# Sums of layer 0 on GpSimd, another join for the last image, and side work that starts only while TensorE has room in a tile

## The chip, the cores and the metric

The kernel runs on one core of a Trainium2 chip. A core has five engines that run their own instruction streams and wait for each other through semaphores: TensorE (PE in the profile, its weight loads PEld), VectorE (DVE), ScalarE (ACT), GpSimd (POOL) and SyncE (SP), whose queue issues the DMA transfers. SBUF is the working memory of 128 partitions; PSUM is the memory that TensorE writes, eight banks of 128 x 512 f32. The metric is the time of one execution on the device in microseconds, the median of several runs. The kernel before takes 18407.37 us, the median of three runs between 18365.60 and 18408.36 us.

## The reference

Four images of 64 x 64 pixels with 96 channels go through four layers. Each layer is `x = x + conv(ln(x))` and then `t = t + ffn(ln(t))`. The "convs" are recurrences along the 4096 pixels of an image.

Layer 0 projects the normalised pixel to a value, a gate, a delta and three sets A, B, C of 96 x 16 numbers, and runs

```python
def step(h, ins):
    A_t, B_t, C_t, d_t, u_t, g_t = ins
    d = d_t[..., None]
    h_new = d * (A_t * h) + d * (B_t * u_t[..., None])
    y = g_t * jnp.sum(C_t * h_new, axis=-1)
    return (h_new, y)
```

so that the sum over the 16 states of a channel, times the gate, is projected to the output. Layers 1 to 3 are selective scans over four orders of the pixels (rows, columns, and both reversed) with 192 inner channels and 16 states:

```python
dA = jnp.exp(dl[..., None] * A)
h = dA * h + (dl * u_l)[..., None] * b_l[:, :, None, :]
y = jnp.einsum('bkdn,bkn->bkd', h, c_l)
...
y = ys[:, 0] + jnp.flip(ys[:, 2], axis=-1) + wh_back(ys[:, 1]) + wh_back(jnp.flip(ys[:, 3], axis=-1))
y = _layernorm(y, out_norm_w, out_norm_b)
y = y * jax.nn.silu(z)
return jnp.einsum('bhwd,cd->bhwc', y, out_proj_w)
```

The sum of the four orders is called the join below. The inputs u and z of a scan come from a projection, a 3 x 3 depthwise convolution and a silu. The ffn multiplies in fp8 with a hidden width of 384.

## The kernel before

**Layer 0** is the function `gated`. An image is cut into 8 strips of 512 pixels, a strip has 12 tiles `i` of 128 rows (32 channels x 4 states; `g` is one of three groups of 32 channels, `q` one of four sets of 4 states). For each tile TensorE projects A and B into one double PSUM bank (`project`, tile name `bc`) and later C into another (`project_c`, PSUM name `c`); VectorE makes the two factors and runs the scan (`recur`); ScalarE copies C with its bias to SBUF, and GpSimd multiplies it with the scan's result (`times_c`, SBUF name `c`). After every three tiles (one `q`, all `g`) `accumulate` has TensorE add the products of 4 states into the PSUM tile `sum`, one matmul with the constant `fold` per tile; after the fourth such round `finish` takes the sum. While tiles are made, the generator `prepare` makes the next strip's normalisation, transposes (`l_xt`) and small projections, three steps per tile, on all engines. From the second image on, the work between layer 0 and layer 1 for image 0 runs beside it as a job.

**The scans** of layers 1 to 3 are the function `scans`. There are 12 stages (3 layers x 4 images), called stage 0 to stage 11 here. A stage has 24 items (2 directions x 4 segments of 1024 pixels x 3 chunks of 128 rows) of 16 states, so 384 tiles of 128 x 1024. For tile `k` VectorE multiplies `bc` (the B row, spread over partitions by TensorE with `sel`, `b_rows`) by `du` and runs the scan to `h`; ScalarE makes the decay `da` two tiles ahead; GpSimd multiplies `h` by the C row `c` that a DMA has brought; TensorE adds the products of tile `k - 3` into `acc` (`accumulate`). For the three states of `ON_POOL` per item GpSimd makes the product that VectorE makes otherwise (tile name `e`), and then VectorE has the scan alone. The double bank `bc` has two buffers, `h` three, `c` six.

**Jobs.** What lies between two layers of an image (`between`: join, norm, gate, output projection, ffn; and then for the next layer the input projection and the convolution) is a Job: generators called chains, three for the first half (`feeds`, `mixers`, `joins`) and two for the second (`convolves`, `takes`). One step of the job, a link below, advances each chain of the current round to its next `yield`. In each scan tile `beside` runs between VectorE's product and its scan, and calls `work`, which adds `rate` to the job's credit and starts as many links as the credit pays. The job of the next image in the stage must be done at tile 356 of 384 of the stage, else it is run to its end there. All jobs stand in one list and run one after another. After layer 3 three images have their ends (`between(im, 3, im.dst)`, first half only) beside the scans, and the last image has its end alone, after all scans, with six PSUM banks.

**Order.** `InOrder` chains every engine's instructions in the order in which the program writes them, so an engine that waits holds all that was written behind. In a tile the order is: carry and decays on ScalarE, `b_rows(k + 1)` on TensorE, `times_c(k - 1)` on GpSimd, VectorE's product, the side work, the scan, then `accumulate(k - 3)` and `keep_busy`. `InOrder` also counts the columns that TensorE streams. `late` in `scans` is the program's own running count of columns by which TensorE is behind, against `FITS` = 7600 columns for a usual tile and `FITS_SHORT` = 4600 for one of `ON_POOL`; before the change it only decides how many dummy matmuls (`keep_busy`, `nothing`) go in.

**The join** (`join_orders`) makes a strip's 512 pixels from four pieces by matmuls with `ident`: per 128 pixels one of `yr`, two of `cols_a`, one of `yc` and four of `part_c`, added up in PSUM. The profile has all helper-issued instructions at line 102, so they are told apart by tile names here. An f32 matmul of the program stands as two in the profile, a transpose as one.

Of the kernel before, what the change touches and what calls it, by code (L numbers as in the profile page):

```python
# [18 lines left out]
HW = 64  # L19
L = HW * HW  # L20
# [109 lines left out]
def metaformer(ctx: ExitStack, tc: tile.TileContext, x, l0_ab, l0_rest, ssm, ffn, out):  # L130
# [227 lines left out]
    def join_orders(im, s, hold):  # L358
# [37 lines left out]
        yield from norm.measure(yt, DI, 1e-5)  # L396
        hold["y", s] = yt, norm

    def mixer_out(im, layer, s, hold):

        w = weights[layer].w
        yt, norm = hold.pop(("y", s))
        zl, zh, xr = load_z(im, s)
        yield from norm.settle()
        yield
        normalise(yt, yt, DI, norm.r, norm.nm)
        yield
        yield True
        g = []
        for i, (a, b, z) in enumerate(((0, 128, zl), (128, 192, zh))):  # L410
            ps = bank("y_c")
            transpose_strip(ps, yt, a, b)
            yield
            v = sb(1, f"u{i}", [128, MM])
            m = b - a
            sc, bias = (w[0:m, W_LN + 2 * i + k : W_LN + 2 * i + k + 1] for k in range(2))
            act.activation(v[0:m], ps[0:m], AF.Identity, bias=bias, scale=sc)
            release()
            yield i == 0
            g.append(v)  # L420
            if i == 0:
                continue
            for v, z, m in ((g[0], zl, 128), (g[1], zh, 64)):
                pool.tensor_tensor(v[0:m], v[0:m], z[0:m], ALU.mult)
                yield
        yield True
        ps = bank("out_proj")
        for q in range(G):
            t = slice(128 * q, 128 * q + 128)
            o = ps[:, C * q : C * q + C]  # L430
            pe.matmul(o, g[0][:, t], w[:, W_OUT : W_OUT + C], start=True, stop=False)
            pe.matmul(o, g[1][0:64, t], w[0:64, W_OUT + C : W_OUT + 2 * C], start=False, stop=True)
            yield
        yield
        x1 = sb(2, "x1", [128, G, C])
        dve.tensor_tensor(x1, xr, ps[:, 0 : G * C].rearrange("p (g c) -> p g c", g=G), ALU.add)
        release()
        yield
        norm = Norm()
        yield from norm.measure(x1, C, 1e-5)  # L440
        hold["x", s] = x1, norm
# [225 lines left out]
    def between(im, layer, dst=None):  # L667


        hold = {"in": {}, "pads": {}, "z": {}}  # L670
        new = dram.tile([L // G, G * C], F32, tag="x", name="x") if dst is None else dst

        def columns():
            return sb(1, "cols_a", [128, L]), sb(1, "part_c", [128, L // 2])

        def first():
            if layer:
                cols_a, part_c = hold["cols"] = columns()
                sp.dma_start(out=cols_a[0:64], in_=im.y[1, 64:128, :])
                sp.dma_start(out=cols_a[64:128], in_=im.y[0, 64:128, :])  # L680
                for k in range(2):
                    sp.dma_start(
                        out=part_c[64 * k : 64 * k + 64],
                        in_=im.y[2, 64:128, k * L // 2 : (k + 1) * L // 2],
                    )
                load_y(im, 0, hold)
            for _ in range(9 if layer else 3):
                yield

        yield [Chain(first())]  # L690
        done = {"y": 0, "x": 0, "end": 0}

        def joins():
            for s in range(NSTRIP):
                yield lambda: done["x"] > s - 2
                yield True
                yield from join_orders(im, s, hold)
                done["y"] += 1

        def mixers():  # L700
            for s in range(NSTRIP):
                yield lambda: done["end"] > s - 2 and (layer == 0 or done["y"] > s)
                if layer:
                    yield from mixer_out(im, layer, s, hold)
                else:
                    yield from measure_x(im, s, hold)
                done["x"] += 1

        def feeds():
            for s in range(NSTRIP):  # L710
                yield lambda: done["x"] > s
                yield from feed_forward(im, layer, s, hold, new)
                done["end"] += 1

        yield [Chain(f()) for f in (feeds, mixers, joins)[: 3 if layer else 2]]
        if dst is not None:
            return

        def second():
            if layer + 1 not in weights:  # L720
                weights[layer + 1] = Weights(layer + 1)
                for _ in range(4):
                    yield
                weights[layer + 1].derive()
                for t in range(0, 15, 3):
                    yield
                    weights[layer + 1].derive_taps(range(t, t + 3))
            im.x = new
            im.u = dram.tile([3, 128, L], F32, tag="u", name="u")
            im.z = dram.tile([DI, L], F32, tag="z", name="z")  # L730
            hold["cols"] = columns()
            hold["in"][0] = load_x(im, 0)
            yield
            yield

        yield [Chain(second())]
        done = {"in": 0, "out": 0}

        def takes():
            for s in range(NSTRIP):  # L740
                yield lambda: done["out"] > s - 3
                yield from take_in(im, layer + 1, s, hold)
                done["in"] += 1

        def convolves():
            yield lambda: done["in"] > 0
            gate_z(im, 0, hold)
            exp_and_ln()
            yield
            yield  # L750
            store_z(im, 0, hold)
            for s in range(NSTRIP):
                yield lambda: done["in"] > min(s + 1, NSTRIP - 1)
                yield True
                yield from convolve(im, layer + 1, s, hold)
                done["out"] += 1

        yield [Chain(f()) for f in (convolves, takes)]

    class Job:  # L760
# [3 lines left out]
            self.rounds, self.rate, self.credit = rounds, rate, 0.0  # L764
            self.chains, self.done, self.round = [], False, -1

        def step(self):
            rate = self.rate[min(self.round, 3)] if isinstance(self.rate, tuple) else self.rate
            self.credit = min(self.credit + rate, 3.0)
            while self.credit >= 1 and not self.done:  # L770
                self.credit -= 1
                while not self.done and all(c.done for c in self.chains):
                    self.chains = next(self.rounds, None)
                    self.round += 1
                    self.done = self.chains is None
                if self.done:
                    break
                for c in self.chains:
                    pump(c)
# [95 lines left out]
    def scans(stages, jobs, pac):  # L875
# [157 lines left out]
        b_from_dram(ON_POOL[0])  # L1033
        working = []

        def work():

            while working and working[0].done:
                working.pop(0)
            if working:  # L1040
                working[0].step()

        late = 0
        for k in range(last + 5):
            q, n = divmod(k, NS)
            if k <= last:
# [7 lines left out]
                if item.chunk == 1 and n == 4 and at(q + 2) is not None:  # L1054
                    if q % per == per - 2:
                        for job in jobs[q // per][:1]:
                            while not job.done:
                                work()
                                settle()
                    segment = Chain(next_segment(items[q + 2 : q + 5]))  # L1060
                if n == 8 and nxt is not None:
# [49 lines left out]
            late = max(0, late + int(pe.columns - begun) - (FITS_SHORT if on_pool(k) else FITS))  # L1111
            settle()
        while working:
            work()
            settle()


    def gated(images, job, pac):
# [158 lines left out]
        def times_c(t):  # L1277
            st, i, h = t["st"], t["i"], t["h"]
            act.copy(st.carry[:, i : i + 1], h[:, MM - 1 : MM])
            c = sb(6, "c", [128, T])[:, 0:MM]  # L1280
            act.activation(c, t["c"], AF.Identity, bias=col(2 * LT + i))
            pool.tensor_tensor(c, h, c, ALU.mult)
            t["h"] = c

        def accumulate(three):

            for t in three:
# [2 lines left out]
                    acc[32 * g : 32 * g + 32],  # L1290
                    fold,
                    t["h"],
                    start=q == 0,
                    stop=q == LQ - 1,
                    tile_position=(0, 32 * g),
                )

# [31 lines left out]
        for k in range(len(tiles) + 2):  # L1329
# [5 lines left out]
                times_c(made[k - 1])  # L1335
            if k > LG and (k - 2) % LG == LG - 1:
                three = [made.pop(j) for j in range(k - 1 - LG, k - 1)]
                accumulate(three)
                if three[-1]["i"] == LT - 1:
                    drain(ending, help_job)  # L1340
                    ending = Chain(finish(three[-1]["st"]))
            for c in (ending, ahead, ahead, ahead):
# [13 lines left out]
    with tc.tile_pool(name="pbig", bufs=2, space=bass.MemoryType.PSUM) as wides_pool:  # L1356
# [5 lines left out]
        for at in range(len(stages)):  # L1362
            jobs.append([])
            if at + 1 < len(stages):
                im, layer = stages[at + 1]
                jobs[-1].append(Job(between(im, layer - 1), (1.75, 1.75, 1.4, 1.4)))

            for im in {10: images[:2], 11: images[2:3]}.get(at, ()):
                jobs[-1].append(Job(between(im, 3, im.dst), 2.6))
        with tc.tile_pool(name="pac", bufs=1, space=bass.MemoryType.PSUM) as pac:  # L1370
            scans(stages, jobs, pac)

# [119 lines left out]
```

## Time and profile before

| | |
|---|---|
| median of three runs | 18407.37 us (18365.60 to 18408.36) |
| profiled execution, its own time | 18376.11 us |
| its span | 18374.3 us |
| layer 0 (to the first scan of stage 0) | about 0 to 1805 us |
| stages 0 to 11 | 1805 to 18160 us |
| the last image's end | 18160 to 18374 us |
| busy, share of the span | DVE 90%, PE 87%, POOL 81%, ACT 59% |

A stage of the scans lasts 1340 to 1370 us, and the last one, stage 11, 1483 us (16677 to 18160). The time that counts in a stage is VectorE's: 312 tiles with a product of 1208 ns and a scan of 2344 ns, and 72 tiles with a scan of 2327 ns. An idle time is attributed in the profile to the instruction that ended it ("bc <- PE bc": VectorE's product waited for TensorE's rows). Idle time of an engine that nobody waits for costs nothing.

### The profile page before, as it was taken

How to read it: one execution, taken by the hardware profiler on the slowest of the kernel's cores; microseconds unless marked ns; L12 is line 12 of the kernel's file. 1: busy time of each engine (PE TensorE's matmuls, PEld its weight loads, DVE VectorE, ACT ScalarE, POOL GpSimd, SP SyncE). 2: the span in 40 equal slices, each digit the busy share in tenths (PEclk: the TensorE clock that was granted, in tenths of full speed). 3: DMA queues.
4: the chain of work that ended last, by engine and by line, in shares of the span. 5: the costliest groups of instructions: out<-in, count | busy, mean ns of one | idle time of the engine just before them, and what ended most of it. 6: DMA issues, size and time to landing. Idle time of an engine off the chain costs nothing. (4 is left out here: it accounts for less than half of the span.)

```text
span 18374.3 us, 238128 instructions
## 1 busy us (share of the span) xinstructions
PE 15921.8 (87%) x76325; PEld 5026.5 (27%) x76325; DVE 16459.7 (90%) x12586; ACT 10918.2 (59%) x18201; POOL 14853.6 (81%) x9319
## 2 busy tenths in 40 slices
PE   8898798798898888898898898898898898888887
PEld 3333222222222322322322222222222222223333
DVE  6756999899999999999999999999999999998885
ACT  3443565565664665665665665665665665666664
POOL 3433888888888988988988988988888988988885
PEclk8998999899899999899999999998899999998887
DMA  2212788788789889889889898898899899898885
GB/s 52 51 48 65 196 220 219 196 223 218 196 224 227 209 220 229 207 226 229 212 224 226 212 228 223 214 225 221 213 230 221 211 228 223 215 230 205 198 213 138
DMA packets 1276076, 3658.88 MB, mean 199 GB/s; under 512 B 287760, under 2 KB 333040, under 8 KB 1268688
## 3 DMA queue, kind: packets, MB, share of 16 engines
q1 hardware_dynamic: 1274256, 3642.86, 79.6%
q8 instruction: 615, 10.08, 0.3%
q14 instruction: 629, 5.15, 0.1%
q10 hardware_dynamic: 576, 0.79, 0.0%
HBM read 3271.50 MB, written 320.86 MB: 196 GB/s over the span
## 5 line engine op out<-in xcount | busy, mean ns | idle before, releaser
L102 POOL TENSOR_TENSOR c<-h,c 128x1024 f32<-128x1024 f32 (+1 forms) x4992 | 11309.7, 2276 | 3032.2 <-DVE h L102 800.2
L102 DVE TENSOR_TENSOR_SCAN h<-da,carry,bc 128x1024 f32<-128x1024 f32 x3744 | 8776.2, 2344 | 558.2 <-POOL c L102 114.6
L102 PE MATMUL acc<-c,twice 64*64 64x512 f32 x36864 | 5449.6, 667 | 77.6 <-POOL c L102 76.9
L102 DVE TENSOR_TENSOR bc<-du,bc 128x1024 f32<-128x1024 f32 x3744 | 4524.2, 1208 | 331.6 <-PE bc L102 294.1
L102 ACT ACTIVATE da<-delta,decay 128x1024 f32<-128x1024 f32 x3744 | 4272.6, 1144 | 534.2 <-DVE h L102 531.2
L102 PE MATMUL bc<-bs,sel 96*128 96x512 bf16 x7488 | 2417.4, 407 | 1708.0 <-DVE h L102 1661.2
L102 ACT COPY carry<-h 128x1 f32<-128x1 f32 x3456 | 654.3, 190 | 3693.1 <-DVE h L102 3683.3
L102 DVE TENSOR_TENSOR_SCAN h<-bc,carry,e 128x1024 f32<-128x1024 f32 x864 | 2010.8, 2327 | 90.4 <-POOL e L102 64.9
L102 POOL TENSOR_TENSOR e<-du,e 128x1024 f32<-128x1024 f32 x864 | 2039.3, 2360 | 60.1 <-DMA e<-cs 59.8
L102 PE MATMUL acc<-sel,nothing 96*128 96x512 bf16 x7653 | 2025.8, 396 | 0.0
L102 PEld LDWEIGHTS acc<-c,twice 64*64 64x64 f32 x36864 | 1063.9, 140 | 2562.3 <-issue 1800.5
L102 PEld LDWEIGHTS <-sel 96*128 96x128 bf16 x7488 | 479.4, 99 | 4560.9 <-DVE h L102 2881.5
L102 ACT ACTIVATE bc<-delta,decay 128x1024 f32<-128x1024 f32 x864 | 963.0, 1115 | 955.7 <-DVE h L102 757.9
L102 PEld LDWEIGHTS <-nothing 96*128 96x128 bf16 x7653 | 646.1, 100 | 1996.7 <-issue 1492.8
L102 ACT ACT_TABLE_LOAD x857 | 1099.5, 1283 | 15.4 <-PEq L1485 0.7
L102 PE MATMUL conv<-pad,tap_lo 128*128 128x512 f32 x1728 | 888.2, 611 | 0.0
L102 ACT ACTIVATE c<-c,l_bias 128x512 f32<-128x512 f32 x384 | 263.8, 687 | 786.2 <-PE c L102 774.3
L102 POOL TENSOR_TENSOR du<-delta,u 128x1024 f32<-128x1024 f32 x288 | 679.9, 2361 | 38.0 <-DMA c<-cs 35.7
L102 PE MATMUL dt_proj<-rows,w 12*128 12x512 f32 x1152 | 670.8, 663 | 1.2 <-ACT hq L102 0.6
L102 PE MATMUL x_proj<-u,xp 128*108 128x512 f32 x1152 | 624.0, 653 | 45.3 <-DMA u<-u 14.2
L102 PE MATMUL conv<-pad,tap_hi 128*128 128x512 f32 (+1 forms) x1152 | 615.3, 630 | 0.0
L102 DVE TENSOR_TENSOR_SCAN h<-da,l_carry,bc 128x512 f32<-128x512 f32 x384 | 491.5, 1280 | 41.5 <-DVE bc L102 1.9
(151 smaller groups left out, 14174.4 us busy)
## 6 DMA issues: line engine op xcount, KB each, us to landing
c<-cs SPq DMA_DIRECT2D x9216, 256.0 KB, 5.5
e<-cs SPq DMA_DIRECT2D x1728, 256.0 KB, 4.8
u<-u SPq DMA_DIRECT2D x288, 512.0 KB, 7.4
y<-y SPq DMA_DIRECT2D x1152, 128.0 KB, 3.4
y<-y SPq DMA_DIRECT2D x144, 512.0 KB, 7.5
xr<-x SPq DMA_DIRECT2D x224, 192.0 KB, 5.8
u<-u SPq DMA_DIRECT2D x288, 128.0 KB, 4.6
pad<-y SPq DMA_DIRECT2D x288, 128.0 KB, 6.1
```

Source lines behind the costliest of these rows:

```text
L102: ins = f(*a, **k).ins
```

## The change

- `times_c` of layer 0 adds the four products of a group on GpSimd into two SBUF tiles that live for the strip (`st.sums`); `accumulate` runs once per strip, with three matmuls instead of twelve.
- The last image's end uses `join_alone`: VectorE adds the pieces in SBUF, reading `cols_a` and `part_c` across, and TensorE transposes the sums, eight transposes per strip. The second half of `part_c` is loaded into two `u` tiles instead, at partitions 0 to 63.
- The other images' ends move: image 0's is listed behind stage 9 (before: 10), image 1's behind stage 10, image 2's behind stage 11 as before.
- A job's link in the scans starts only while `late`, the tile's columns so far and 2048 columns for `accumulate` are within `FITS` or `FITS_SHORT`; credit that is not spent is kept up to 5 (before 3). Where the program waits for a job to end, the limit is off.
- Rates go from 1.75 and 1.4 links per tile (first and second half) to 2.2 and 1.7, in stages 9 and 10 to 2.6 and 2.4, and for the ends from 2.6 to 2.8.

```diff
+    def join_alone(im, s, hold):
+        yr, yc = hold["in"].pop(s)
+        if s + 1 < NSTRIP:
+            load_y(im, s + 1, hold)
+        cols_a, part_c = hold["cols"]
+        rows = slice(SR * s, SR * s + SR)
+        def across(v):
+            return v.rearrange("p (c r) -> p r c", r=HW)[:, rows, :]
+        def along(v):
+            return v.rearrange("p (r c) -> p r c", c=HW)
+        dve.tensor_tensor(along(yr), along(yr), across(cols_a), ALU.add)
+        c0 = 0
+        for v in [part_c[0:64]] + [u[0:64] for u in hold["rest"]]:
+            w = v.shape[1] // HW
+            part = along(yc)[:, :, c0 : c0 + w]
+            dve.tensor_tensor(part, part, across(v), ALU.add)
+            c0 += w
+        yield
+        yt = sb(2, "yt", [128, G, DI])
+        for pair in range(2):
+            ps = bank("y_t")[:, 0 : 2 * DI].rearrange("p (g c) -> p g c", g=2)
+            for g in range(2):
+                t = slice(128 * (2 * pair + g), 128 * (2 * pair + g) + 128)
+                pe.transpose(ps[:, g, 0:128], yr[:, t], ident)
+                pe.transpose(ps[:, g, 128:DI], yc[:, t], ident[0:64, 0:64])
+            yield
+            act.copy(yt[:, 2 * pair : 2 * pair + 2, :], ps)
+            release()
+            yield pair == 0
+        norm = Norm()
+        yield from norm.measure(yt, DI, 1e-5)
+        hold["y", s] = yt, norm
...
+        alone = dst is not None and im is images[-1]
...
-                for k in range(2):
+                for k in range(1 if alone else 2):
                     sp.dma_start(
                         out=part_c[64 * k : 64 * k + 64],
                         in_=im.y[2, 64:128, k * L // 2 : (k + 1) * L // 2],
                     )
+                if alone:
+                    hold["rest"] = [sb(4, "u", [128, T]) for _ in range(2)]
+                    for k, u in enumerate(hold["rest"]):
+                        t = L // 2 + k * T
+                        sp.dma_start(out=u[0:64], in_=im.y[2, 64:128, t : t + T])
...
-                yield from join_orders(im, s, hold)
+                yield from (join_alone if alone else join_orders)(im, s, hold)
...
-        def step(self):
+        def step(self, full=lambda: False):
             rate = self.rate[min(self.round, 3)] if isinstance(self.rate, tuple) else self.rate
-            self.credit = min(self.credit + rate, 3.0)
-            while self.credit >= 1 and not self.done:
+            self.credit = min(self.credit + rate, 5.0)
+            while self.credit >= 1 and not self.done and not full():
...
-        def work():
+        def work(hurry=False):
             while working and working[0].done:
                 working.pop(0)
             if working:
-                working[0].step()
+                working[0].step((lambda: False) if hurry else crowded)
+
+        def crowded():
+            most = FITS_SHORT if on_pool(k) else FITS
+            return late + int(pe.columns - begun) + 4 * MM > most
...
                             while not job.done:
-                                work()
+                                work(True)
...
             act.copy(st.carry[:, i : i + 1], h[:, MM - 1 : MM])
-            c = sb(6, "c", [128, T])[:, 0:MM]
+            g, q = divmod(i, LQ)
+            if i == 0:
+                st.sums = [sb(6, "c", [128, T]) for _ in range(2)]
+            total = st.sums[g // 2][:, g % 2 * MM : g % 2 * MM + MM]
+            c = total if q == 0 else sb(6, "c", [128, T])[:, 0:MM]
             act.activation(c, t["c"], AF.Identity, bias=col(2 * LT + i))
             pool.tensor_tensor(c, h, c, ALU.mult)
-            t["h"] = c
+            if q:
+                pool.tensor_tensor(total, total, c, ALU.add)
+            t["h"] = total
...
-                    start=q == 0,
-                    stop=q == LQ - 1,
+                    start=True,
+                    stop=True,
...
-                accumulate(three)
                 if three[-1]["i"] == LT - 1:
+                    accumulate(three)
                     drain(ending, help_job)
...
-                jobs[-1].append(Job(between(im, layer - 1), (1.75, 1.75, 1.4, 1.4)))
-            for im in {10: images[:2], 11: images[2:3]}.get(at, ()):
-                jobs[-1].append(Job(between(im, 3, im.dst), 2.6))
+                jobs[-1].append(Job(between(im, layer - 1), (2.6, 2.6, 2.4, 2.4) if at >= 9 else (2.2, 2.2, 1.7, 1.7)))
+            for im in {9: images[:1], 10: images[1:2], 11: images[2:3]}.get(at, ()):
+                jobs[-1].append(Job(between(im, 3, im.dst), 2.8))
```

More of the change, by code (lines that the diff above doesn't have):

```diff
@@ L1113, in scans @@
         while working:
-            work()
+            work(True)
             settle()
```

## The prediction

> **What bounds the kernel now.** First the busy time by stretches (duration, busy us and instruction counts of PE, PEld, DVE, ACT and POOL, granted TensorE clock, DMA share, GB/s): layer 0, stages 0 to 2, 3 to 9, 10, 11, the last image's end.
>
> ```profile
> 0.00:1805.00 1805.00, 1610.85 (x4170) 635.52 (x4170) 1167.39 (x1699) 729.46 (x1664) 656.40 (x1142) 0.91 0.21 52
> 1805.00:5867.00 4062.00, 3443.98 (x16406) 934.37 (x16405) 3775.38 (x2473) 2417.02 (x3785) 3455.58 (x1854) 0.93 0.85 212
> 5867.00:15307.00 9440.00, 8264.97 (x41805) 2520.12 (x41805) 8912.94 (x6283) 5904.31 (x9539) 8248.37 (x4719) 0.93 0.89 221
> 15307.00:16677.00 1370.00, 1197.94 (x6186) 382.18 (x6184) 1278.87 (x939) 864.95 (x1420) 1189.69 (x706) 0.93 0.90 222
> 16677.00:18160.00 1483.00, 1243.74 (x6895) 447.21 (x6887) 1300.06 (x1060) 895.15 (x1546) 1250.99 (x788) 0.85 0.83 203
> 18160.00:18374.00 214.00, 160.32 (x881) 107.13 (x880) 25.11 (x137) 107.33 (x249) 52.57 (x113) 0.55 0.26 62
> ```
>
> Layer 0 is TensorE's (1611 of 1805 us). Stages 0 to 10 are VectorE's (93 to 94%), so only its idle time can go there. Stage 11, with two and a half ends of images beside its scans, has VectorE at 88% and lasts 140 us longer than stage 9. The last end has TensorE busiest, at a clock of 0.55.
>
> Then the waits: of VectorE in all scans (total us, times, longest), and behind the dots in layer 0, VectorE's and then TensorE's.
>
> ```profile
> DVE bc L102 <- PE bc L102: 294.1, 226, 5.7
> DVE h L102 <- POOL c L102: 118.8, 31, 14.2
> DVE st L102 <- DMA xr<-x: 98.3, 22, 9.7
> DVE h L102 <- POOL e L102: 65.4, 33, 12.0
> DVE st L102 <- ACT yt L102: 18.1, 7, 9.6
> DVE x L102 <- PE out_proj L102: 14.5, 13, 3.8
> ...
> DVE da L102 <- PE bc L102: 320.4, 153, 9.8
> ...
> PE l_xt L102 <- ACT bs L102: 78.4, 31, 10.5
> ```
>
> About 294 us is all that TensorE's lateness costs the scans. Last the groups by shape (busy us, mean ns, idle before), the final three from the last end alone.
>
> ```profile
> L102 PE MATMUL sum<-c,fold 128*32 128x512 f32 x768 | 139.7, 610 | 0.9 <-POOL c L102 0.9
> L102 POOL TENSOR_TENSOR c<-h,c 128x512 f32<-128x512 f32 x384 | 486.7, 1267 | 1040.4 <-ACT c L102 572.1 <-ACT l_carry L102 279.7 <-DVE bc L102 187.2
> L102 DVE TENSOR_TENSOR x<-xr,out_proj 128x384 f32<-128x384 f32 x96 | 52.2, 543 | 63.9 <-PE out_proj L102 39.6 <-issue 24.2
> ...
> L102 PE MATMUL y_t<-ident,pad 128*128 128x128 f32 x64 | 24.0, 478 | 22.7 <-DMA pad<-y 22.7
> L102 PE MATMUL y_t<-ident,cols_a 128*64 128x128 f32 x128 | 23.5, 465 | 0.0
> L102 PE MATMUL y_t<-ident,pad 64*128 64x64 f32 x64 | 20.9, 426 | 0.0
> ```
>
> **A, layer 0's sums.** TensorE loses 96 of 128 groups of three fold matmuls (32 strips, one group of four stays). The row gives 139.7 / 128 = 1.09 us per group, so 96 x 1.09 = 105 us of the engine that bounds. GpSimd gains 32 x 9 adds of 1.267 us, 365 us, beside 656 of 1805: room by the total. But the adds stand in GpSimd's order ahead of the next strip's norm (three passes per strip, which `prepare` needs before `l_xt`), and TensorE already waits 78.4 us there. Nothing: 0; all three passes late by an add: 32 x 3 x 1.27 = +122. I take one add per strip, +41, because the other two passes lie a tile or more ahead. The fold at the strip's end comes 1.27 us later, behind six matmul instructions of 0.43 us that TensorE has first: 0 (cover gone: +41). Sum -64, between -105 and +17.
>
> The Trainium skill, "GPSIMD Engine Reference", section Engine selection, speaks against this part: elementwise work belongs on VectorE, GpSimd being about half as fast on two inputs. The rows agree on the ratio (1267 ns for 512 columns against 543 for 384) but show GpSimd idle for 1149 us of layer 0. By the page, with all 365 us on the path, A would be +260; by the rows it is the -64 above.
>
> **B, the last join.** Per strip TensorE now runs 64 instructions on `y_t`; in a steady strip of 20.4 us the chain has 6.0 + 1.0 + 1.1 = 8.1 us of them. Eight transposes of about 0.27 us (the timeline's four `ff_xt` take 1.0 to 1.1 us at this clock) are 2.2. So 5.9 us x 7 strips = -41, and at the first strip 9.65 becomes 2.2 us plus four VectorE adds of 1024 elements together: 1.45 us by 543 ns for 384, 2.7 if reading across costs what ScalarE's copy into `cols_a` costs (1085 against 578 ns): -5. In the other strips VectorE is idle and hides the adds. One more DMA load goes into SP's queue at the start, 0.6 us by its neighbours there: +2 with the landing. ScalarE's 107.3 / 8 = 13.4 us per strip bounds the gain at 8 x 7 = -56; adds on the path of every strip would leave -46 + 8 x 2.7 = -24. I take -44.
>
> **C, links with a limit.** Counting links tile by tile in the two programs: the same work takes tiles 7 to 342 in stages 4 to 8 before and 5 to 326 after; all jobs meet tile 356 but stage 10's, whose last links come 13 in one tile. The three ends take 123, 118 and 122 tiles before and 152, 149 and 159 after, spread from stage 9's tile 302 to stage 11's tile 282. Before, each tile of a job has 1 or 2 links (2 or 3 in the ends). After, 43 tiles of a stage have none and 18 have 5.
>
> C1, TensorE less late. The program's mean `late` falls from 1090 to 608 columns in stages 4 to 9 and from 3308 to 674 in stage 11. Of the 294 us, 84 fall between 16500 and 18000 us. There I take 54 away, since `late` falls to a fifth but short stalls at small `late` stay; of the other 210 a third, 70, because the waits before stand at tiles with `late` below 1000 as often as above. C1 = -124, between 0 and -294.
>
> C2, VectorE's own side work too close behind its source. VectorE's `st <- yt` (statistics of a joined strip) stands a tile behind ScalarE's copy today; after, 71 of these statements stand in the tile of the copy (6 of 8 in stages 3 to 8, all in stages 10 and 11). In such a tile ScalarE must first do carry 0.19, decay 1.14, often delta 0.67, and the copy 0.47 = 2.5 us from the end of the last scan, while VectorE arrives after its product, 1.21. The wait is 1.3 us; with `normalise` of another strip (4 x 0.54) ahead it is 3.4, and with more side work up to 4.6. Listing each of the tiles this way gives 1.7 on average: +120. Stage 11's 18.1 + 13.2 for the same two kinds of wait go out of this: +89. Lower end 71 x 0.6 - 31 = +12, upper end 71 x 4.6 - 31 = +296.
>
> C3, GpSimd and DMA. Bunched links put two gate products (2 x 1.27 us) and two ffn adds (2 x 0.92) nearer together, and 118.8 + 65.4 us of waits on GpSimd exist already. A load of `measure_x` stands with its statistics in one tile once in each of stages 0 to 2, about 3 us each above today's 4.5. Both: +25 (0 to +90, half as much again). Stages 9 and 10 carry more, stage 11 less, of the same work: 0, as the sum over stages counts.
>
> C = -124 + 89 + 25 = -10.
>
> The Trainium skill, "TensorE: Matmul & The Clock Gate", Part 1, says that an idle window of some 3.4 us halves the clock; tiles without links could do that. In the rows the clock is 0.93 in the stages and 0.85 in stage 11, where TensorE is the most crowded by the program's count, so crowding did not keep it up. If all stages fell to 0.85, C1 would be gone and the sum some 124 higher.
>
> **Sum.** -64 - 44 - 10 = -118 on the profiled execution's 18376: 18258. That execution lies 31 us below the median of the three runs and 11 above the fastest; with 12 for that I say 18270.
>
> **Rivals.**
> 1. The bunched links win (slower). Waits like C2 cost 4.6 us each, as where two links of other chains are ahead on ScalarE: +296 in place of +89, and C3 +70. Sum -64 - 44 - 124 + 296 + 70 = +134: 18522. It passes zero at 3.3 us a wait. For: VectorE has no slack in a stage, and stage 11's waits of this kind were up to 9.6 us long, 2.6 on average. Against: TensorE, less late, delivers `y_t` sooner.
> 2. GpSimd's adds delay layer 0's norms wholly: A = +17, total 18351. For: the 78.4 us at `l_xt`. Against: GpSimd's idle 1040 us before its products.
> 3. The limit takes most of TensorE's waits (-234 of 294) and VectorE's waits are at their lower end (+12, C3 0): C = -222, 18058. For: stage 11's 84 us. Against: the waits at small `late`.
> 4. The limit does little: `late` counts columns, not time, and C1 is -30. Total 18364. For: in stages 0 to 2 the largest `late` (5428 on average over an item) stands in tiles of the convolution where VectorE waits for nothing.
>
> **How the numbers follow.** The forecast has 0.45, the rivals 0.13, 0.15, 0.12 and 0.15. A measurement tells 0.3%, 55 us, from no change: faster is below 18352. The forecast, rival 3 and most of rivals 2 and 4, which stand at that line, make faster 0.70, same 0.17, slower 0.13. The range reaches from between forecast and rival 3, 18110, to between rivals 4 and 1, 18440; within the forecast alone, 18180 to 18360.
>
> **What would show it.** A: the group `sum<-c` has 192 instructions and layer 0 ends near 1740 us; `l_xt <- ACT bs` grows from 78 to about 120. B: after the last scan 170 us remain, with `y_t` at 64 transposes. C1: `bc <- PE bc` in the scans falls below 200. C2: `st <- ACT yt` rises from 18 to over 100 us with some 70 times; stage 11 lasts 1400 us or less and stage 9 longer than 1340. Wrong if these waits exceed 240 us, or if layer 0 does not shrink.

## The result, and the profile after

The changed kernel takes 18866.71 us (median of five runs, 18852.55 to 18875.08), against 18407.37 us before: the ratio is 1.0255, with a 95% interval of 1.0244 to 1.0266. The forecast of 18270 us was wrong in sign, and the time lies above the forecast's range (18110 to 18440 us). The profiled execution has a span of 18861.5 us and a mean granted clock of 0.895 (before 18374.3 us and 0.918).

By stretches, with the columns of the same view of before (duration; busy us and instruction counts of PE, PEld, DVE, ACT, POOL; clock; DMA share; GB/s): layer 0, stages 0 to 2, 3 to 8, 9, 10, 11, and the last image's end.

```profile
0.00:1787.00 1787.00, 1541.22 (x3592) 624.60 (x3592) 1164.28 (x1698) 725.48 (x1663) 1017.65 (x1429) 0.90 0.21 52
1787.00:5869.00 4082.00, 3483.23 (x16376) 940.89 (x16376) 3775.70 (x2471) 2417.28 (x3784) 3452.82 (x1853) 0.92 0.85 211
5869.00:14247.00 8378.00, 7271.77 (x35762) 2221.84 (x35760) 7651.52 (x5387) 5066.95 (x8180) 7071.35 (x4044) 0.90 0.86 213
14247.00:15740.00 1493.00, 1283.82 (x6339) 415.59 (x6340) 1290.38 (x974) 890.40 (x1481) 1201.88 (x733) 0.86 0.83 205
15740.00:17244.00 1504.00, 1269.05 (x6307) 412.69 (x6305) 1290.37 (x981) 903.80 (x1511) 1208.25 (x745) 0.87 0.82 204
17244.00:18661.00 1417.00, 1195.76 (x6465) 391.82 (x6461) 1285.33 (x944) 812.67 (x1335) 1212.69 (x693) 0.89 0.83 205
18661.00:18861.50 200.50, 119.19 (x428) 71.27 (x424) 42.02 (x168) 107.65 (x249) 62.44 (x113) 0.52 0.27 66
```

Layer 0 is 17 us shorter and the last end 13, the way that was meant but far less than forecast (64 and 44); all the loss lies between, from 1787 to 18661 us. The scans take 517 us more: stages 0 to 2 some 8 each, 3 to 8 some 47, stage 9 149 and stage 10 135; stage 11 takes 71 less. VectorE's busy time in the scans is nearly the same (15267 us before, 15293 after), so nearly all of the 517 us are waits. VectorE's waits in the scans of the changed kernel (total us, times, longest):

```profile
DVE bc L102 <- PE bc L102: 559.8, 315, 13.1
DVE h L102 <- POOL c L102: 113.0, 28, 8.0
DVE h L102 <- ACT bc L102: 104.3, 56, 4.1
DVE h L102 <- POOL e L102: 82.7, 37, 17.8
DVE st L102 <- ACT yt L102: 74.3, 42, 5.1
DVE x L102 <- PE out_proj L102: 70.3, 31, 6.5
DVE st L102 <- DMA xr<-x: 51.3, 20, 7.8
DVE st L102 <- POOL xh L102: 47.0, 39, 3.0
```

More than half of the loss is the first line, 294.1 before: VectorE waits for TensorE's rows twice as long, although the program's count says that TensorE is half as late. `h <- ACT bc` has grown most for its size: the scan of a short tile (one of `ON_POOL`) waits for the decay that ScalarE makes. In the kernel before it and the last line are small:

```profile
DVE h L102 <- ACT bc L102: 14.3, 10, 4.1
DVE st L102 <- POOL xh L102: 8.2, 10, 2.9
```

In what follows, **loss** is VectorE's time above an undisturbed tile: the spacing of two scans' ends less 3.605 us (for an `ON_POOL` tile 2.376 us), the spacing where no link runs. Most short tiles stand at 2.24 us rather than at 2.376, so the level of the loss is some 10 us per stage too low in every kernel; only its differences between kernels count. Mean loss per stage, in us, of all profiled kernels that use one setting throughout:

| kernel | time | ratio to before | stages 0-2 | 3-8 | 9 | 10 | 11 |
|---|---|---|---|---|---|---|---|
| before | 18407 | 1 | 58 | 53 | 48 | 74 | 192 |
| changed | 18867 | 1.0255 | 66 | 100 | 197 | 209 | 120 |
| sums and join alone | 18373 | 0.9982 | 68 | 57 | 54 | 82 | 192 |
| limit alone | 19050 | 1.0351 | 57 | 124 | 128 | 140 | 177 |
| rates and ends alone | 18858 | 1.0249 | 93 | 96 | 202 | 196 | 56 |
| changed, two links at most | 18615 | 1.0115 | 39 | 79 | 90 | 318 | 77 |
| before, every second tile | 19182 | 1.0425 | 96 | 135 | 130 | 145 | 189 |
| changed, more dummies | 18842 | 1.0242 | 68 | 97 | 172 | 209 | 119 |
| limit, two links, old rates | 18669 | 1.0143 | 55 | 93 | 83 | 100 | 86 |
| lower rates, limit in 0-2 | 18485 | 1.0045 | 40 | 87 | 77 | 98 | 166 |
| best | 18284 | 0.9936 | 38 | 55 | 59 | 92 | 168 |

### The profile page after: what moved, and what is told of

The parts are those of the page before. It is cut to its first block, busy times and chain, and to the rows that moved or that the text cites. A ratio compares the mean times of both kernels' runs of the same rounds, so it can differ in the third digit from the quotient of the medians.

```text
span 18861.5 us, 236302 instructions
## 1 busy us (share of the span) xinstructions
PE 16164.0 (86%) x75258; PEld 5078.7 (27%) x75258; DVE 16499.6 (87%) x12618; ACT 10924.2 (58%) x18201; POOL 15227.1 (81%) x9607
## 5 line engine op out<-in xcount | busy, mean ns | idle before, releaser
L102 PE MATMUL acc<-c,twice 64*64 64x512 f32 x36864 | 5574.0, 681 | 78.8 <-POOL c L102 78.5
L102 PE MATMUL bc<-bs,sel 96*128 96x512 bf16 x7488 | 2467.4, 414 | 1558.3 <-DVE h L102 1504.9
```

What stands on the lines that cost most here:

```text
L102: ins = f(*a, **k).ins
```

## The experiments

The theory after the first reading was bunching: the kept credit lets up to five links start in one tile, and in-order engines then wait for each other in turn. Its rivals were the higher rates, the empty tiles that let TensorE's clock fall (0.918 to 0.895), and the moved ends. Four runs take these apart.

**Sums and join alone** (`times_c`, `accumulate`, `join_alone` as in the change; the rest of before).

> The kernel before with the sums of layer 0 and the last join alone; links, rates and ends as before. The two stand at the two ends of the span, so one run shows both, and the scans between them are a control: first scan's end to last scan's end stays at 16356 us within 15. By the prediction the first scan ends at 1740 us (-64) and the last image's end takes 170 us (-44): some 18300 us in the median. By the profile of the changed kernel the first is -17 and the second -13: some 18377 us. If the changed kernel's links had spoilt these two parts, this run shows the larger gains.

Measured: 18373.33 us, ratio 0.9982 (0.9971 to 0.9993). The first scan ends at 1766 us (-39) and the last end takes 200.9 us (-13). Over the eight profiled kernels that have the new sums the first scan ends at 1779 us on average, over the six without at 1809, so the sums give some 30 us; the -17 in the changed kernel was at the low side of a scatter of some 15 us. The last end is 201 us in both. Nothing of the two was spoilt by the links. The control missed: the scans took 16421 us, 65 more than before with the same program in them. A single profile's stages are no better than that, which the later readings allow for by means over stages and kernels.

**The limit alone.**

```diff
-            self.credit = min(self.credit + rate, 3.0)
-            while self.credit >= 1 and not self.done:
+            self.credit = min(self.credit + rate, 5.0)
+            while self.credit >= 1 and not self.done and not full():
...
```

(The rest of the limit is `crowded` and `work(True)`, as in the change.)

> The kernel before with the limit and the credit of 5 alone; rates, ends, layer 0 and last join as before. At these rates the jobs of stages 3 to 10 no longer end by themselves and some 42 links are run in tile 355, so tiles 0 to 351 of a stage are compared, by VectorE's time above an undisturbed tile: stages 4 to 8 have 49.8 us of it before and 101.0 in the changed kernel. Bunching (my theory: tiles with 3 to 5 links make the engines wait for each other in turn): 38 such tiles against 72 in the changed kernel, so 70 to 85 us, and VectorE's bc<-PE bc above 400 us in all. Higher rates (rival): near 50 us. Empty tiles that cool TensorE (rival): 40 of 43 such tiles are there, so 95 to 100 us and a granted clock of 0.90 in the stages. The time: 18850, 18620 and 19000 us, with 25 us for each run of 42 links.

Measured: 19050.04 us, 1.0351 (1.0323 to 1.0378). Tiles 0 to 351 of stages 4 to 8 lose 85 us, as bunching said, and `bc <- PE bc` is 586.5 us. The clock of 0.901 fits the rival of the empty tiles as well; its 95 to 100 us do not. The total is 200 us above bunching's: the links left over at tile 355 make a loss of 347 us in tiles 352 to 383 of stages 3 to 10, and the third end, 96 links short, makes the last end 295 us. So at the old rates the limit leaves the jobs unfinished, and the 643 us that this kernel loses are in good part these leftovers.

**Rates and ends alone** (`2.2, 2.2, 1.7, 1.7`; `2.6, 2.6, 2.4, 2.4` in stages 9 and 10; ends at 9, 10, 11 with 2.8; no limit, credit 3).

> The kernel before with the higher rates and the moved ends alone, no limit, credit to 3. No tile of a job is empty and none has over 3 links. Bunching by the limit: stages 4 to 8 stay at 50 to 60 us above the undisturbed tiles (the program's late rises from 1090 to 2024 columns). Higher rates (rival): about 100 us as in the changed kernel. Stages 9 and 10, at 2 to 3 links in nearly every tile and a late of 12514 columns, go the way of stage 11 before, 1487 us each by both; if the moved ends are what cost stages 9 and 10 of the changed kernel their 149 and 135 us, it shows here without a limit. Stage 11 falls to 1400 us or less. In all 18690 us by bunching, 18910 by the rates.

Measured: 18857.62 us, 1.0249 (1.0228 to 1.027). Stages 4 to 8 lose 94 us over tiles 0 to 351, not 50 to 60: here bunching by the limit fails as the one cause. Without any limit the whole loss of the changed kernel is there, and stages 9 and 10 take 1497 and 1492 us, stage 11 1351. VectorE's waits in its scans:

```profile
DVE bc L102 <- PE bc L102: 660.9, 429, 6.2
DVE h L102 <- POOL e L102: 108.1, 27, 17.7
DVE x L102 <- PE out_proj L102: 90.5, 42, 6.6
DVE h L102 <- POOL c L102: 81.0, 23, 6.6
DVE h L102 <- ACT bc L102: 58.6, 39, 3.6
```

They are shorter (6.2 us the longest, 13.1 in the changed kernel) and more (429 against 315). The two settings of the change thus make the same loss in two manners: in tiles 0 to 351 of stages 4 to 8 the rates lose 94 us and the limit 85, both together 101, the kernel before 50. By the medians rates and ends alone cost 451 us; both settings with sums and join cost 460, and as sums and join give 33, both settings together 493. The limit adds some 42 us to what the rates and ends cost alone.

**The changed kernel with two links per tile at most** (`and begun < 2` in the loop of `step`).

> The changed kernel with one more condition: no tile begins more than two links (the limit, the kept credit, rates, ends, layer 0 and the last join are as in it). 54 tiles of a stage are empty, more than the 43 of the changed kernel, and none has 3 or more. Bunching: stages 4 to 8 fall from 101 us above the undisturbed tiles (tiles 0 to 351) to 60 or less, and bc<-PE bc from 560 to 320 us or less. Empty tiles that cool TensorE (rival): still 95 us or more, with a clock of 0.90. Stage 10 is no clean comparison: its job is behind at tile 355 and 203 links are run there at once, some 170 us. In all about 18480 us by bunching, 18750 by the clock.

Measured: 18614.78 us, 1.0115 (1.0097 to 1.0134). Stages 4 to 8 lose 66 us over tiles 0 to 351 (101 in the changed kernel, 50 before; 60 or less was expected), with 54 empty tiles and a clock of 0.909: taking the bunches away gives back two thirds, and the empty tiles do little. `bc <- PE bc` is 576.4 us, of which one wait of 197.8 is stage 10's run of 203 links; 379 remain, above the 320 expected. Unlooked for, stages 0 to 2 lose only 39 us, 19 less than before. There one wait had fallen, that of the statistics for their load: VectorE in stages 0 to 2 of this kernel,

```profile
DVE bc L102 <- PE bc L102: 59.3, 42, 3.4
DVE st L102 <- DMA xr<-x: 25.1, 15, 3.9
```

against 52.4 and 98.3 us in the kernel before, where this wait has its whole 98.3 us in these three stages.

These runs suggested another theory, density: that only the number of links per tile, as a mean over a few tiles, counts. The next four runs try it against bunching and the clock.

**Every second tile** (the kernel before; `while now and self.credit >= 1`, with `now` true where `k % 2 == 0`; credit to 6).

> The kernel before with its links begun in every second tile only (credit kept up to 6): no limit, the rates and so the mean density of before, but 177 empty tiles of a stage and 161 tiles with 3 or 4 links. Bunching within a tile: by the changed kernel's rows (0.53 us above an undisturbed tile for 3 or 4 links, 0.2 for fewer) tiles 0 to 351 of stages 4 to 8 go from 50 to some 105 us, in all over 19100 us. Density (the theory after the first four runs: what counts is the number of links per tile, as a mean over a few tiles, whether higher rates or the limit make it): they stay at 60 us or less; with 24 to 38 links run at once in tile 355 of eight stages, 18600 us. Empty tiles that cool TensorE: the granted clock falls under 0.90 and the time rises with it, over 19000 us.

Measured: 19181.57 us, 1.0425 (1.0411 to 1.0439); tiles 0 to 351 of stages 4 to 8 lose 101 us. That is bunching's 105, and density alone falls: at an unchanged mean rate, three or four links in one tile and none in the next double the loss. The clock, 0.899, also fell as the rival of the empty tiles said; this run alone does not part the two, the next one does. The first half of the job (join, gate, ffn) in one stage of before (stage 6), and then of this kernel (stage 5), VectorE's two largest waits:

```profile
DVE bc L102 <- PE bc L102: 8.4, 7, 2.4
DVE h L102 <- POOL c L102: 5.5, 1, 5.5
```

```profile
DVE bc L102 <- PE bc L102: 33.3, 20, 5.5
DVE x L102 <- PE out_proj L102: 6.2, 3, 2.3
```

**More dummy matmuls in the changed kernel** (`FILL = 3584` for 2048).

> The changed kernel with room for 3584 instead of 2048 columns of dummy matmuls per tile (922 of them in a stage instead of 599); links and everything else as in it. Clock (a cooler TensorE is the cause: 0.90 against 0.93, with TensorE busy 195 us longer in stages 3 to 8 for the same work): the granted clock comes back to 0.92 or more, stages 3 to 8 fall from 100 us above the undisturbed tiles to 60 or 70, and the time to some 18550 us. Density or bunching: the clock may rise, but the stages stay at 100 us or above; 18870 to 18950 us.

Measured: 18842.28 us, 1.0242 (1.0226 to 1.0259). The mean clock, from the view of cores, of the changed kernel and of this one:

```profile
core 0: 18861.5 us, clock 0.895
```

```profile
core 0: 18831.2 us, clock 0.923
```

The clock is above that of the kernel before (0.918), and stages 3 to 8 lose 97 us, as without. So the fallen clock is a companion of the loss: bringing it back is worth 24 us of 459. The Trainium skill ("TensorE: Matmul & The Clock Gate", Part 1) says that the clock follows how busy TensorE has been; the rise with the dummies agrees, and the time does not follow.

**The limit with two links at the old rates** (with sums and join).

> The limit with at most two links per tile, at the rates and ends of before, with the new sums of layer 0 and the new last join. Against the limit alone this takes away the tiles with 3 to 5 links and nothing else in the stages; against two links at the higher rates it lowers the rates. Tiles 0 to 351 of stages 4 to 8: bunching 50 us (from 85); density 55 to 60, since 41 empty tiles press the same links into fewer tiles, and in any case under the 66 us of the higher rates; if the limit costs by itself, 66 or more. Stages 0 to 2 near 39 us as with two links before (58 in the kernel before). Stage 11 ends with 163 links at once, some 120 us. In all some 18530 us.

Measured: 18668.70 us, 1.0143 (1.0129 to 1.0157). Tiles 0 to 351 of stages 4 to 8 lose 64 us, against 85 for the limit alone: taking away the bunches of 3 to 5 gives 21 us. But 64 is nearly what two links gave at the higher rates (66), and some 14 us above the kernel before; it lies between what density allowed (55 to 60) and the bound for a cost of the limit itself (66 or more), nearer to the latter. Under this limit the rate hardly sets the pace any more: the first half of a job takes 194 tiles here and 197 there. Stages 0 to 2 lose 55, not 39. Stage 11's leftover of 163 links makes the last end 342 us.

**Lower rates from stage 3 on** (`1.6, 1.6, 1.5, 1.5`; the limit with two links in stages 0 to 2; in the last end `(dve if alone(im, layer) else pool).tensor_tensor` for products and ffn adds).

> A kernel put together from what the runs showed: the new sums of layer 0; in stages 0 to 2 the limit with at most two links per tile at the higher rates (39 us above the undisturbed tiles there, against 58); in stages 3 to 10 no limit and lower rates, 1.6 and 1.5, which fill the stage to tile 355; the new last join, and in the last end the gate products and the two adds of the ffn on VectorE instead of GpSimd. Density: stages 4 to 8 at 40 to 50 us (50 before). If it is bunching alone that costs, they stay at 50. The last end: if its chain now goes through GpSimd's 2.8 + 0.9 us per strip, it falls from 201 to some 175 us; if not, 200. In all 18240 us, 18290 if only stages 0 to 2, layer 0 and the join gain.

Measured: 18485.04 us, 1.0045 (1.0033 to 1.0058), slower than before. Stages 0 to 2 hold their 40 us, but tiles 0 to 351 of stages 4 to 8 lose 72 instead of 40 to 50. The last end is 197 us, 4 less: GpSimd's products and adds were not what bounds it.

**A rate for each stage.** Density was refuted as the only cause and now missed at a low rate; the rival was that a rate is good or bad by which links meet. One kernel with seven rates for the first half, and one with their order reversed (`first = {3: 1.65, 4: 1.7, ...}.get(at, 1.75)`).

> The kernel before with one rate per stage for the first half of the job: 1.65, 1.7, 1.75, 1.8, 1.9, 2.0 and 2.2 links per tile in stages 3 to 9, the second half at 1.4 throughout. Read is VectorE's time above an undisturbed tile while the first half runs: 36 and 40 us at 1.75 in two kernels, 53 at 1.6, 66 at 2.2 with 1.7. Density: it rises steadily with the rate, 35 at 1.65, 45 to 50 at 1.9, 55 at 2.0, 66 at 2.2. Phase (rival: the rate decides which links meet the three short tiles of an item and each other, and 1.75 is a good meeting): 1.7 and 1.8 already cost 50 or more, with no order in the rest. The total is 18450 to 18550 us by both.

> The same rates in the reverse order of stages, 2.2 in stage 3 to 1.65 in stage 9, so that each rate is seen in two stages. Density: the same curve as in the other order, within 8 us at each rate. Phase: the same ragged values again at the same rates. If the two orders disagree at a rate by more than 15 us, neither is shown and the differences between stages are those of single executions.

Measured: 18526.83 us (two runs; 1.0067, 1.0041 to 1.0093) and 18497.46 us (1.0052, 1.0034 to 1.0071). Loss while the first half runs, us:

| links per tile | 1.65 | 1.7 | 1.75 | 1.8 | 1.9 | 2.0 | 2.2 |
|---|---|---|---|---|---|---|---|
| rates rising with the stages | 32 | 48 | 40 | 43 | 58 | 54 | 74 |
| rates falling | 41 | 41 | 42 | 44 | 50 | 57 | 79 |

Both orders give one curve, flat to 1.8 and then steep, apart by 9 us at most. Up to 2.0 no tile has more than two links, so the rate costs by itself, without bunches: density holds from 1.8 on. The 52 us in the first half at 1.6 stay outside this curve, in seven stages of one kernel; its links take 197 tiles, as many as 1.65 takes at 32 and 41 us. The rival of the meeting links could make this; it was not tried at 1.6, and the cause is open.

**The best.** Sums, join, the limit with two links in stages 0 to 2 alone, the rates of before from stage 3 on, ends at 2.3.

> The new sums of layer 0 and the new last join; in stages 0 to 2 the limit with at most two links per tile at 2.2 and 1.7; from stage 3 on no limit and the rates of before, 1.75 and 1.4; the ends of the images at 2.3 instead of 2.6, so that they fill stage 11 to tile 369; in the last end the products and adds on VectorE, which gave 4 us. Layer 0 -30, stages 0 to 2 -57, the last end -17 against the kernel before; stages 3 to 10 as before; stage 11 by density 176 us above the undisturbed tiles instead of 192. In all 18290 us. If 1.75 and 1.4 were good only beside what stood ahead of them, stages 3 to 8 lose some 20 us each and it is no faster than before.

Measured: 18284.31 us, 0.9936 (0.9919 to 0.9953), 0.6% below the kernel before and 3% below the changed one. VectorE's largest waits in its scans:

```profile
DVE bc L102 <- PE bc L102: 344.2, 248, 6.0
DVE h L102 <- POOL c L102: 110.0, 31, 15.9
DVE h L102 <- POOL e L102: 47.5, 26, 10.7
DVE st L102 <- DMA xr<-x: 24.0, 13, 4.2
```

The gain over sums and join alone lies in stages 0 to 2, 37.6 us of loss each for 68 (58 in the kernel before), and most of it is the load's wait, 24.0 us for 101.4. It takes the rates and the limit together: the load's wait in these stages is 52.4 us with the higher rates alone and 56.5 with two links and the limit at the old rates, and both lose more elsewhere (93 and 55 us of loss per stage). Stage 11 loses 168 us for 192 at 2.3 links in place of 2.6.

**Where the join's gain went.** In the last end TensorE's clock was 0.55 and is 0.52 with the new join, 0.50 in its steady strips. The last run puts dummies ahead of TensorE's work there, where it waits.

> The best kernel so far (18284 us) with three dummy matmuls of 512 columns into each bank of y_t, y_c and ff_h just before the real work, in the last image's end alone. Its strips take 19.1 us there at a granted clock of 0.50, and TensorE waits some 5 us of each for pad, yt and xq. Cold TensorE (theory for the missing gain of the last join: with fewer matmuls the clock fell from 0.56 to 0.50, so every step on TensorE takes twice its time): the clock there rises to 0.7 or more, a strip takes 16 us or less, and the last end falls from 197 to 175 us or less. Chain through all engines (rival): the clock may rise, but strips stay at 18.5 us or more. If the clock stays at 0.5, the 21 dummies of a strip, some 9 us, lengthen it to 22 us or more, and the last end to 220 us or more. The rest of the span is as before.

Measured: 18306.72 us, 0.9953 (0.9935 to 0.997). The last end of the best kernel, and of this one:

```profile
18077.40:18274.90 197.50, 119.90 (x440) 71.74 (x436) 60.22 (x201) 107.23 (x249) 26.73 (x81) 0.52 0.28 67
```

```profile
18082.40:18295.70 213.30, 146.66 (x608) 79.15 (x604) 60.65 (x200) 107.91 (x249) 26.18 (x81) 0.66 0.25 62
```

In the steady strips the clock rises to 0.72, and a strip takes 20.4 us instead of 19.1. So the dummies do not pay, and no busy column comes near the end's length: a strip is a chain through all engines. But the run does not settle whether a cold TensorE is what made it long, since the dummies themselves stand in the chain. Part of one strip on TensorE:

```profile
18199.95 1.46 PE L102 MATMUL y_t<-sel,nothing 96*128 96x512 bf16 x3
18201.20 1.42 PE L102 MATMUL y_t<-ident,pad 128*128 128x128 f32 x4
18202.55 1.46 PE L102 MATMUL y_c<-sel,nothing 96*128 96x512 bf16 x3
18203.81 1.06 PE L102 MATMUL y_c<-ident,yt 128*128 128x128 f32 x4
```

Followed back through this strip (18187.0 to 18207.4 us), the chain holds 4.0 us of dummies and 5.4 us of TensorE's other work; in a strip of the best kernel (18173.5 to 18192.6 us) it holds 9.8 us of TensorE's work. What a warm clock without dummies in the chain would give is open.

## Why the prediction was wrong, step by step

**A, layer 0's sums (-64).** Some -30 (-17 in the changed kernel). The groups by shape in the run of sums and join alone, and one of TensorE's waits in its layer 0:

```profile
L102 PE MATMUL sum<-c,fold 128*32 128x512 f32 x192 | 53.7, 647 | 16.0 <-POOL c L102 16.0
L102 POOL TENSOR_TENSOR c<-c 128x512 f32<-128x512 f32 x288 | 363.9, 1264 | 22.6
```

```profile
PE l_xt L102 <- ACT bs L102: 80.5, 31, 10.4
```

There are 192 instructions, as said, and the 288 adds take the 364 us counted. But these 192 fold instructions cost 53.7 us, where a quarter of 139.7 is 35: the cut is 86 us, not 105. The delay of the norms, +41, did not come at all (78.4 to 80.5 us), nor did rival 2. In its place TensorE waits longer for the sum (0.9 to 16.0 us), for ScalarE's copy of C (7.2 to 17.2) and for VectorE's scans (57.6 to 65.5): with less work it meets its neighbours sooner. Against A the prediction had set +260, all adds on the path; they lay in GpSimd's idle time instead (its busy time in layer 0 went from 656 to 1018 us). The Trainium skill ("GPSIMD Engine Reference", section 4.1 Engine selection) puts elementwise work on VectorE rather than on GpSimd; here, with GpSimd idle, the adds on it did not lengthen layer 0.

**B, the last join (-44).** -13. Two groups by shape in the last end of the changed kernel:

```profile
L102 PE MATMUL y_t<-ident,pad 128*128 128x128 f32 x32 | 15.0, 469 | 38.1 <-DVE pad L102 33.8 <-issue 4.2
L102 DVE TENSOR_TENSOR pad<-pad,cols_a 128x512 f32<-128x512 f32 x8 | 8.6, 1073 | 27.0 <-DMA pad<-y 26.8 <-issue 0.2
```

`y_t` has 64 transposes in all, as said, and the four adds take 2.4 us of VectorE per strip (1.07 for the one shown), within the 1.45 to 2.7 given; the join is off TensorE. But the step "5.9 us x 7 strips" took TensorE's busy time for the chain. Steady strips went from 20.4 to 19.5 us, 0.9 less where 5.9 was counted, since the chain goes on through statistics, norm, transposes, gate and projection; the first strip gave its 5 us. The -24 of the range's inner end was still too large. Relieving GpSimd shortened it by 4 us more, and dummies on TensorE lengthened it.

**C1, TensorE less late (-124).** This is the step that failed: `bc <- PE bc` rose by 266 us, beyond every bound given. The step read the program's `late`, 1090 columns to 608, as TensorE's real delay. The runs show no such tie: with a mean `late` in stages 4 to 6 of 1090, 608, 2024 and 538 (before, changed, rates and ends, two links at old rates), the first halves of stages 4 to 8 lose 36, 71, 66 and 53 us. (The prediction gives 1090 and 608 for stages 4 to 9; over these the two kernels' counts are 1133 and 650, which changes nothing in the argument.) `late` counts columns and supposes that TensorE streams them without a stop. A link also holds TensorE in order behind ScalarE and GpSimd: in the first half of one stage TensorE waits for `xh` and `u` in the changed kernel,

```profile
PE out_proj L102 <- POOL u L102: 6.9, 4, 3.2
PE ff_xt L102 <- ACT xh L102: 6.3, 2, 4.0
```

where the same half of before has 0.5 us of the first and none of the second. That such waits pass on to `b_rows` is argued from the order; no run took one alone away, so this part of the cause is not shown. What the runs do show is that the higher rates alone bring the loss (94 us in tiles 0 to 351 of stages 4 to 8, for 50), and that bunches of links bring it too (101 us at the old mean rate). The prediction gave the rates themselves no price: C had only their effect on `late`.

**C2, VectorE's side work (+89).** Near in size, by luck in part, since the mix is another. `st <- ACT yt` in the scans went from 18.1 to 74.3 us and `x <- PE out_proj`, a wait for TensorE and not for ScalarE, from 14.5 to 70.3, together +112. The mean wait for ScalarE is 1.8 us (forecast 1.7), but 42 statements wait and not 71.

**C3, GpSimd and DMA (+25).** `h <- POOL c` and `e` together went up by 11 us, `st <- POOL xh` by 39. The load's wait, priced as a loss in stages 0 to 2, fell from 98.3 to 51.3 us. `h <- ACT bc`, +90 us, was in no term: ScalarE has the links' normalisations and copies ahead of a short tile's decay.

"Stages 9 and 10 carry more, stage 11 less, of the same work: 0" failed as well: stages 9 and 10 took 149 and 135 us more and stage 11 gave 71 back, so a term put at nothing is 213 of the 517 us. The run without limit shows the same three (+154, +122, -136), so this comes with the rates and the moved ends, which no run parts in these stages; stages 3 to 8 have no ends, and there it is the rates. Stage 11 was expected at 1400 us or less and takes 1417; in the run of rates and ends it takes 1351.

**Rival 1** had the sign but not the mechanism: its waits of 4.6 us on ScalarE did not come (1.8 us), and the sum it gave, 18522, lacks TensorE's 390 us (from -124 to +266).

## What to carry to other kernels

A program's count of an engine's work can pace side work, but it does not measure the engine's delay: it leaves out the waits that the side work itself brings, and here the loss rose while the count halved. Judge side work by the loss per tile against its rate: here it stayed flat from 1.65 to 1.8 links per tile and then grew, with one kernel at 1.6 outside the curve, and the same links in bunches cost twice at the same mean rate. Apply a limit only in the stages where it pays, and read there which wait it took away; in stages 0 to 2 it paid only together with the higher rates, and what went was the wait for a load, which may be had in a simpler way that was not tried.

## What was not expected of the hardware

The granted clock of TensorE moved without the time: 0.895 to 0.923 with 24 us less, of 18867. In the last end dummies raised it from 0.50 to 0.72 and each strip took 1.3 us more, with the dummies in its chain. The Trainium skill says of transposes ("TensorE: Matmul & The Clock Gate", Part 4) that they do not count as work that keeps the clock up; the last end, rich in transposes, agrees with its 0.50 and with the rise by ordinary matmuls. But TensorE also stands idle there (busy 119.9 of 197.5 us), which may keep the clock down as well, and no run took the transposes alone away.
